# Two transformer layers with a mixture of experts: the order of all engines' instructions from another model of time

## The chip, the cores and the metric

The kernel runs on one core of a Trainium2 chip, in fp32. A core has five engines, each of which takes its own queue of instructions in order: TensorE (PE, with a separate queue for weight loads, PEld), VectorE (DVE), ScalarE (ACT), GpSimd (POOL) and SyncE (SP), which here issues most of the DMAs. The metric is device time in microseconds for one execution; a profile of one execution stands beside it.

## What is computed

The input is x of 4 batches x 512 tokens x 256. The two layers have this form (function bodies cut to what matters):

```python
# layer 0
xn = layernorm(x)
q, k, v = xn @ Wq.T + bq, xn @ Wk.T + bk, xn @ Wv.T + bv
context = (elu(q) + 1) * cumsum((elu(k) + 1) * v, axis=1) * SCALE
n0 = rms(xn) * norm_w
logits = n0 @ Wc.T / clip(temperature, 0.1)             # 512 genes
top_vals, top_idx = top_k(logits, 32)
expressed = sum(softmax(top_vals) * genes[top_idx])
x = x + context @ Wo.T + bo + tanh(expressed @ Wd.T) * n0 * (expressed @ Wu.T) * scale
# layer 1
xn = layernorm(x)
q, k, v = split(rms(xn) @ w_qkv.T)
w = exp(rms(k))
y = sigmoid(rms(q)) * (cumsum(w * v) / (cumsum(w) + 1e-6))
u, g = split(y @ w_swiglu.T)
x = x + xn + (u * silu(g)) @ w_out.T                    # hidden width 1024
scores = softmax(xn @ gate_w.T)                          # 16 experts, 2 are chosen
x = x + sum over the 2 experts of scores * swiglu(xn @ w_gate_up[e]) @ w_down[e]
      + swiglu(xn @ shared_gate_up) @ shared_down
```

All cumulative sums run along the 512 tokens of a batch.

## The kernel before

The 2048 tokens are 16 tiles of 128. The whole kernel is one function, `tile_two_layers`. It is made of generators, each of which writes a part of the program between two `yield`s:

- `layer0(b, i0, nt)`: layer 0 for nt tiles of batch b. Statistics and normalised rows (L201 to L214), their transposes on PE (`turn`, L221), logits of the genes (L289), four rounds of MAX8 and MATCH_REPLACE over 512 logits a tile on DVE for the 32 largest (L301, L302), the attention's products (`project`, L244), its elu and its cumulative sum (L257 to L280), the gene products (`express`, L316 to L334) and the output product with the residual add (L339, L342).
- `mix(b, i0, nt)`: the attention of layer 1 up to y, called yT (products L384, cumulative sums L421, yT L432), and the scores and the two chosen experts of each token (L435 to L456).
- `dense(busy)`: what depends on no routing: 8 halves of a batch (256 tokens), each of 11 chunks of hidden columns: three of the shared expert (from xn1T) and eight of the attention's swiglu (from yT). A chunk has four products into `gu` (L576), ACT and DVE or POOL work into `hid` (L580 to L587), and two products into `acc` (L596), issued two chunks behind. After the 11th, `acc` is added to x, which is kept on chip as `xs` (L607).
- `route()`: numbers of the rows in which each token's two copies stand, sorted by expert (products L486 and L487, then DVE). `scatter()`: 32 indirect DMAs from GpSimd that put the normalised rows into `xrows` in DRAM (L544). `load_experts()`: the experts' weights, into `wex`.
- `experts()`: 24 pairs of row tiles (47 tiles), each with its expert's number in a register: rows fetched (L711), transposed (L703), up products `pu` (L740), silu and product into `hb` (L748, L749), transposed again, down products `py` (L761), copied and written to `yrows` in DRAM (L770, L772).
- The tail: 32 indirect DMAs from GpSimd gather the rows of `yrows` into `ys` (L806), DVE adds them to `xs` with their weights (L817), and SP writes the output (L821, L826).

The order in the program comes from `together`, which takes steps from several generators in proportion to their lengths:

```python
    together(a(0, 0, 2))                                  # a is layer0, m is mix, d(n) is n steps of dense
    together(m(0, 0, 2), a(0, 2, 2))
    together(m(0, 2, 2), a(1, 0, 4), d(NC))               # NC = 11
    together(m(1, 0, 4), a(2, 0, 4), d(NC))
    together(m(2, 0, 4), a(3, 0, 4), d(NC))
    together(m(3, 0, 4), d(NC), (load_experts(), 17))
    together((route(), 8), d(5))
    together((scatter(), 33), d(14))
    run_all(islice(dd, 2 * NC - 19))                      # three more
    together((experts(), NP2 + 2))
    for step, _ in enumerate(dd):                         # the last 22 chunks, with gathers and adds between
```

So the program's text holds 66 of the 88 chunks ahead of the experts and 22 behind them, beside the gathers. The scatters, the expert weight loads and the gathers are `paced`: each depends on the `acc` product last written in the program, so that transfers are spread over the dense parts.

This text is not yet the order in which the engines run. The framework, Tile, collects the instructions with their dependencies (on data, and on the buffers of pools: three for `gu`, one for `acc`, four PSUM banks `pm` for the two layers, two for `pu`, one each for `pt` and `py`). At the end of a block a list scheduler goes through a model of time: when an engine is free, it gets, of the instructions whose inputs are ready in that model, the one that stands first in the program. The order found so is written into the engines' queues, with semaphores for the dependencies. On the chip the queues run in order: an instruction that waits holds up those behind it. In the kernel before, the model is the framework's default one, which the kernel doesn't choose.

Of the kernel before, what the change touches and what calls it, by code (L numbers as in the profile page):

```python
# [53 lines left out]
def tile_two_layers(  # L54
# [21 lines left out]
    out: bass.AP,  # L76
):
    nc = tc.nc
    V, S, G, T = nc.vector, nc.scalar, nc.gpsimd, nc.tensor

    const = ctx.enter_context(tc.tile_pool(name="const", bufs=1))
# [794 lines left out]
```

## Time and profile before

| | us |
|---|---|
| median of 3 runs | 591.41 (590.49 to 591.55) |
| the profiled execution's own time | 591.42 |
| its span, first to last instruction | 589.7 |
| PE busy by dense gu products (L576), from yT and from xn1T | 127.5 and 47.3 |
| PE busy by acc products (L596) | 67.4 |
| PE busy by pu (L740) and py (L761) of the experts | 63.8 and 44.5 |
| DVE busy by MAX8 (L301), 48 of its 64 | 32.9 |
| POOL busy by 32 scatters (L544) and 32 gathers (L806) | 31.0 and 30.7 |
| mean granted clock of PE | 0.975 of full |

How to read it: busy times of matmuls are sums of pipelined records, whose ends are modelled; they tell shares rather than limits. A group of instructions names the line of the kernel, the engine, the operation, what is written and what is read. "idle before" with a releaser says what ended the wait ahead of an instruction. An engine's idle time matters only where the chain of work that ends last runs through it. On that chain, followed back from the last instruction, PE has 61% of the span, DVE 21%, ACT 6% and POOL 4%.

### The profile page before, as it was taken

The page shows a single profiled execution, that of the slowest core. Times are in us where ns is not written, and L with a number is a line of the kernel's source. Part 1 is how long each engine was busy: PE and PEld are TensorE (multiplying, and loading weights), DVE is VectorE, ACT ScalarE, POOL GpSimd, SP SyncE. Part 2 cuts the span into 40 slices and gives each one's busy share as a digit, 9 for nine tenths or more (in the row PEclk, how much of TensorE's full clock was granted, in tenths as well). Part 3 has the DMA queues.
Part 4 walks back from the last instruction along what each step waited for, and adds up shares of the span by engine and source line. Part 5 has one row for each costly group of instructions (what it writes and reads, how often), then busy time and mean ns, then how long its engine had stood idle before and what let it go on. Part 6 is the DMA issues. An engine that isn't in the chain of part 4 may idle for free.

```text
span 589.7 us, 7350 instructions
## 1 busy us (share of the span) xinstructions
PE 539.4 (91%) x2384; PEld 393.0 (67%) x2384; DVE 373.1 (63%) x992; ACT 232.6 (39%) x528; POOL 173.9 (29%) x214
## 2 busy tenths in 40 slices
PE   3557989989999999999999999969999999999987
PEld 1334656558565685656877778857777777788876
DVE  3979999997896797967943785322222222235563
ACT  1453746653555625556265311103333333321111
POOL 1234232353221432224440326661000000006651
PEclk9788999999999999999999999989999999999999
DMA  4993000000000000000075602224233333114441
GB/s 159 375 377 140 1 1 1 2 0 1 1 1 0 1 1 1 1 1 1 1 236 170 182 2 80 91 86 136 90 108 107 108 108 98 55 63 125 126 133 46
DMA packets 38453, 47.39 MB, mean 80 GB/s; under 512 B 4016, under 2 KB 34960, under 8 KB 38160
## 3 DMA queue, kind: packets, MB, share of 16 engines
q1 hardware_dynamic: 35344, 38.53, 20.0%
q0 software_dynamic: 3072, 8.39, 4.6%
q8 instruction: 20, 0.33, 0.2%
q14 instruction: 17, 0.14, 0.1%
HBM read 28.30 MB, written 18.61 MB: 80 GB/s over the span
## 4 chain that ended last, share of the span: by engine, by line
PE 61%; DVE 21%; ACT 6%; POOL 4%; issue 3%; DMA 2%; SPq 0%; another core or an unknown queue 0%; POOLq 0%; ACTq 0%; DVEq 0%
PE gu L576 16%; PE pu L740 9%; PE acc L596 9%; PE py L761 7%; PE pm L384 5%; DVE rep L302 4%; DVE top L301 4%; PE pt L703 3%; POOL xrows L544 3%; PE pm L244 3%; PE pm L289 2%; PE pm L221 2%; PE pm L339 2%; DVE sums L430 2%; DVE sums L421 1%
## 5 line engine op out<-in xcount | busy, mean ns | idle before, releaser
L576 PE MATMUL gu<-yT,wugt 128*128 128x256 f32 x512 | 127.5, 385 | 0.0
L576 PEld LDWEIGHTS gu<-yT,wugt 128*128 128x128 f32 x512 | 96.0, 192 | 19.5 <-issue 7.2
L580 ACT ACTIVATE th<-gu 128x256 f32<-128x256 f32 (+1 forms) x88 | 33.0, 382 | 133.4 <-PE gu L576 85.9
L806 POOL DMA_INDIRECT ys<-yrows,slot x32 | 30.7, 961 | 145.4 <-PE gu L576 130.1
L596 PE MATMUL acc<-wot,hid 128*128 128x256 f32 x256 | 67.4, 386 | 5.9 <-DVE hid L584 5.5
L582 DVE SCALAR_TENSOR_TENSOR th<-th,gu 128x256 f32<-128x256 f32 (+1 forms) x88 | 36.1, 412 | 55.0 <-ACT th L580 46.3
L740 PE MATMUL pu<-wex,xgT 128*128 x188 | 63.8, 461 | 0.8 <-DMA xg<-xrows 0.8
L587 POOL TENSOR_TENSOR hid<-hid,th 128x256 f32<-128x256 f32 (+1 forms) x44 | 34.3, 782 | 101.1 <-ACT hid L586 97.8
L596 PEld LDWEIGHTS acc<-wot,hid 128*128 128x128 f32 x256 | 48.4, 192 | 15.5 <-DVE hid L584 5.9
L244 PE MATMUL pm<-xnT,wqkv 128*128 128x512 f32 (+1 forms) x120 | 46.7, 529 | 4.1 <-ACT lg L293 1.8
L576 PE MATMUL gu<-xn1T,sgu 128*128 128x256 f32 (+1 forms) x192 | 47.3, 382 | 1.4 <-ACT hid L586 1.3
L749 DVE TENSOR_TENSOR hb<-pu,hb 128x176 f32<-128x176 f32 x47 | 16.1, 342 | 51.0 <-ACT hb L748 51.0
L384 PE MATMUL pm<-w,xn1T 128*128 128x512 f32 (+1 forms) x128 | 45.7, 501 | 0.0
L761 PE MATMUL py<-wex,hgT 128*128 x188 | 44.5, 379 | 0.0
L761 PEld LDWEIGHTS py<-wex,hgT 128*128 128x128 f32 x188 | 35.6, 190 | 8.6 <-issue 0.2
L576 PEld LDWEIGHTS gu<-xn1T,sgu 128*128 128x128 f32 (+1 forms) x192 | 33.8, 181 | 9.5 <-ACT hid L586 2.6
L740 PEld LDWEIGHTS pu<-wex,xgT 128*128 128x128 f32 x188 | 32.0, 190 | 11.0 <-ACT xgT L717 1.0
L384 PEld LDWEIGHTS pm<-w,xn1T 128*128 128x128 f32 x128 | 24.6, 193 | 21.4 <-issue 17.9
L244 PEld LDWEIGHTS pm<-xnT,wqkv 128*128 128x128 f32 x120 | 23.8, 202 | 22.0 <-issue 13.2
L753 DVE COPY hgT<-pt 128x512 f32<-128x512 f32 (+1 forms) x24 | 16.3, 681 | 34.2 <-PE pt L703 34.2
L544 POOL DMA_INDIRECT xrows<-xn,slot x32 | 31.0, 969 | 23.8 <-DVE cpair L538 9.9
L301 DVE MAX8 top<-rep 128x8 f32<-128x512 f32 x48 | 32.9, 686 | 0.4
(162 smaller groups left out, 881.5 us busy)
## 6 DMA issues: line engine op xcount, KB each, us to landing
xrows<-zero SPq DMA_DIRECT2D x1, 6016.0 KB, 22.6
xg<-xrows SPq DMA_DIRECT2D x23, 256.0 KB, 2.7
yrows<-yg SPq DMA_DIRECT2D x23, 256.0 KB, 2.1
wex<-in_w_gate_up_dram SPq DMA_DIRECT2D x8, 704.0 KB, 4.8
xs<-in_x_dram SPq DMA_DIRECT2D x4, 512.0 KB, 7.7
wugt<-in_wug_dram SPq DMA_DIRECT2D x1, 2048.0 KB, 12.3
wex<-in_w_down_dram SPq DMA_DIRECT2D x4, 512.0 KB
out_dram<-xs SPq DMA_DIRECT2D x7, 256.0 KB, 2.7
```

Source lines behind the costliest of these rows:

```text
L244: T.matmul(pm, wqkv[:, h, c * P : (c + 1) * P], xnT[:, h, 0:W], start=(h == 0), stop=(h == NH - 1),)
L301: V.max(tp[:, 8 * r : 8 * r + 8], src)
L384: T.matmul(o[:, 0:n], xnT[:, h, i * P : (i + 1) * P], w1[:, h, at : at + n], start=(h == 0), stop=(h == NH - 1),)
L544: sc = G.indirect_dma_start(out=xrows, out_offset=bass.IndirectOffsetOnAxis(ap=slot[:, k, i : i + 1], axis=0), in_=xn1[:, i // NT, i % NT] ...
L576: T.matmul(gu[0:m, k], w[:, h, at : at + m], ins[which][:, h], start=(h == 0), stop=(h == NH - 1))
L580: S.activation(th[0:m], gu[0:m, 0], AF.Tanh, scale=0.5)
L582: V.scalar_tensor_tensor(th[0:m], th[0:m], 1.0, gu[0:m, 0], ALU.add, ALU.mult)
L587: G.tensor_tensor(hid[0:m], hid[0:m], th[0:m], ALU.mult)
L596: mm = T.matmul(acc[:, t], hid[0:m, t * P : (t + 1) * P], dw[0:m, dc], start=(n == 0 and t == 0), stop=(n == NC - 1), skip_group_check=True,)
L740: T.matmul(pg[:, 0 : 2 * NI], xT[:, i, h], wex[:, bass.ds(at[i] + h * 2 * NI, 2 * NI)], start=(h == 0), stop=(h == NH - 1),)
L761: mm = T.matmul(py[:, i * D : (i + 1) * D], hT[:, i, h], wex[:, bass.ds(at[i] + EW - (2 - h) * D, D)], start=(h == 0), stop=(h == 1),)
L806: G.indirect_dma_start(out=ys[:, asked], out_offset=None, in_=yrows, in_offset=bass.IndirectOffsetOnAxis(ap=slot[:, k, n : n + 1], axis=0) ...
```

## The change

One call is added at the start of `tile_two_layers`:

```diff
@@ -76,6 +76,8 @@
     out: bass.AP,
 ):
     nc = tc.nc
+
+    ctx.enter_context(tc.block(schedule_with_timeline_sim=True))
     V, S, G, T = nc.vector, nc.scalar, nc.gpsimd, nc.tensor
```

It puts the whole function into a block whose instructions are scheduled with the framework's finer model, a simulation of the time line, in place of the default one. The rule (of what is ready, the earliest in the program) stays, and so do the instructions, their operands, the pools and the dependencies. What differs is when the model holds an engine to be free and an input to be ready, and with that which instruction it picks: chunks of `dense` stand last in each stage's text but need no routing, so they are what fills an engine that has nothing earlier ready. The result is another order in each engine's queue. Line numbers of the changed kernel are higher by two.

## The prediction

> **What bounds the kernel now.** I read the page's first part, then busy time by stage, then the timeline around the last expert pair and at the end, and last the orders of the two programs.
>
> ```profile
> span 589.7 us, 7350 instructions
> PE 539.4 (91%) x2384; PEld 393.0 (67%) x2384; DVE 373.1 (63%) x992; ACT 232.6 (39%) x528; POOL 173.9 (29%) x214
> ```
>
> TensorE (PE) is idle for 50.3 us of 589.7. The stages say where (columns: stretch, its length, busy time and count of PE, PEld, DVE, ACT, POOL, granted clock, DMA share, GB/s):
>
> ```profile
> 0.00:86.00 86.00, 56.89 (x217) 34.73 (x218) 72.23 (x237) 38.30 (x84) 23.95 (x41) 0.88 0.51 180
> 86.00:145.00 59.00, 57.07 (x252) 37.84 (x251) 56.11 (x153) 31.87 (x70) 24.25 (x31) 1.00 0.00 1
> 145.00:219.00 74.00, 71.99 (x316) 48.45 (x314) 62.03 (x152) 39.03 (x89) 23.37 (x29) 1.00 0.00 1
> 219.00:299.00 80.00, 77.47 (x339) 52.23 (x338) 67.63 (x174) 43.33 (x94) 26.03 (x28) 1.00 0.05 14
> 299.00:345.00 46.00, 43.74 (x190) 32.03 (x189) 23.83 (x61) 20.57 (x55) 13.25 (x20) 1.00 0.55 166
> 345.00:406.00 61.00, 55.47 (x244) 47.17 (x243) 25.44 (x67) 7.34 (x20) 32.26 (x35) 0.94 0.23 80
> 406.00:526.00 120.00, 119.04 (x572) 90.92 (x571) 33.02 (x73) 43.79 (x96) 0.00 (x0) 1.00 0.31 97
> 526.00:590.00 64.00, 57.69 (x266) 49.65 (x265) 32.84 (x79) 8.34 (x23) 30.75 (x32) 0.98 0.35 101
> ```
>
> The start loses 29 us of PE; after it PE is 97% busy with VectorE (DVE) close behind (84 to 95%) up to 299 us. Then come the last mix, route and scatter (345 to 406), the experts, and a tail of 64 us in which PE still works 57.7. That work hides the gathers of the expert rows, which begin only after the last expert row is written (columns: start, us, engine, line):
>
> ```profile
> 525.65 0.37 ACT L770 COPY yg<-py 128x256 f32<-128x256 f32 x1 [1.36 <-PE py L761]
> ...
> 529.31 0.98 POOL L806 DMA_INDIRECT ys<-yrows,slot  x1 [128.23 <-PE gu L576]
> ...
> 548.48 0.94 POOL L806 DMA_INDIRECT ys<-yrows,slot  x1 [0.30 <-issue]
> 549.73 0.94 POOL L806 DMA_INDIRECT ys<-yrows,slot  x1 [0.30 <-issue]
> ...
> 576.28 0.95 POOL L806 DMA_INDIRECT ys<-yrows,slot  x1 [0.40 <-PE acc L596]
> ...
> 579.54 0.48 DVE L817 SCALAR_TENSOR_TENSOR xs<-ys,cpair,xs 128x256 f32<-128x256 f32 x1 [0.93 <-DMA ys<-yrows,slot]
> ...
> 585.54 0.69 DVE L607 TENSOR_TENSOR xs<-acc,xs 128x512 f32<-128x512 f32 x1 [1.29 <-PE acc L596]
> ```
>
> To see: 3.9 us from the last down product (its matmul ends near 525.4) to the first gather; 1.25 us from gather to gather when nothing holds them; 3.3 us from the last gather to its add; 3.5 us from the end of the last residual add (586.2) to the end. The gathers alone take 31 x 1.25 = 38.8 us, which today lie beside dense matmuls.
>
> **What the Trainium skill says.** "DMA: Bandwidth & Descriptors", section "SWDGE vs HWDGE vs iDMA": for a DMA issued from GpSimd, software on that engine computes the descriptors. The trace agrees: POOL is held 0.95 us a gather. "TensorE: Matmul & The Clock Gate", section "Part 1: The HAM clock gate": after an idle window of about 3.4 us matmuls run at half clock until some 3.4 us of work have passed. The trace agrees: four acc records that elsewhere span 1.03 us took 2.07 after an idle of 5.46.
>
> ```profile
> 394.83 2.07 PE L596 MATMUL acc<-wot,hid 128*128 128x256 f32 x4 [5.46 <-DVE hid L584]
> ```
>
> **The change, part by part.** Every instruction is kept but for six more activation-table loads (1.28 us each, on an engine that is 39% busy: nothing taken; 7.7 us if all stood on the path). SP's queue keeps its order but for the expert weight loads among themselves (8.4 MB that have over 60 us to land), POOL's that of scatters and gathers. What moves is the dense layer. A chunk is four gu and two acc products: eight gu records in 1.73 us and four acc records in 0.865, so 2.595 us of PE; there are 88. Each matmul at its back-to-back spacing in this trace (0.865 us for 512 columns, 0.595 for 352, 0.46 for 272, 0.4325 for 256, 0.11 for a 128-wide transpose) gives 517.5 us of work in either kernel. "Lag" is the time at a landmark less the work issued before it. Before: first logits of batch 1 done, 85.9 - 46 = 40; last turn of batch 2's rows, 144.7 - 100.9 = 44; of batch 3's, 219.0 - 172.2 = 47; last mix, 298.9 - 247.8 = 51; route products, 344.6 - 289.0 = 56; first expert product, 407.4 - 342.4 = 65; last matmul, 585.5 - 517.5 = 68. Then 4.2 us to 589.7.
>
> Chunks issued before these landmarks, old and new order: batch 2, 11.3 and 14.5; batch 3, 22.3 and 25.5; last mix, 35.0 and 50.8; route, 45.3 and 63.5; first expert product, 65.3 and 84.7. The old order keeps nearly two halves (57 us) for behind the experts. The new one puts its last three chunks between the first expert pairs and nothing behind the last down product: PE has 18 chunks, 47 us, more to do before route, and none in the tail.
>
> Tail: 3.9 + 38.8 + 3.3 + 0.5 (add) + 0.7 (last residual add, now behind the gathered adds) + 3.5 = 50.7 us with PE empty. The adds, 0.48 us, fit between gathers; the dense products that pace the gathers are long done. Bounds: 41 if the 0.30 gaps vanished, 54 if landings slow.
>
> Start, to 86 us: DVE sets it. Two tiles' top-32 are interleaved, and statistics and normalising of other batches stand ahead of batch 0's mix; they filled waits behind it before. Three chunks run in PE's gaps. I take the lag as it was, 40, bounds 34 to 44.
>
> Batch 1: five chunks stand ahead of the first tile's transposes and five more ahead of the third tile's logits. Work up to these is 84.6 us, 38.6 after the landmark at 46; at 1.02 (PE's busy 206 us against 202 of work from 86 to 299) that is 86 + 39 = 125, where DVE got them at 104.7. DVE then has rows of 38.7 us by mean duration; over the kernel those rows sum to 429 against 373 busy, 0.87, so 33.7 us, against 25 us of PE almost without chunks (the second half's yT is not made). End at 126 + 33.7 = 159.7 with 109.0 done: lag 51 for 44.
> Batch 2, the same: 39 x 1.02 = 40 to the logits, 1 to DVE, then 44.4 x 0.87 = 38.6 of DVE against 32 of PE: 239 with 179.8 done, lag 59 for 47.
> Batch 3: 25 chunks are free and the order takes them, so PE is full for 82.6 x 1.02 = 84 us up to the turns of q and k (323); then 18 us of DVE to the last out product and 8 to the normalised rows, with 23 us of PE inside: 349.5, 288.9 done, lag 61.
> Last mix: 47.3 of PE against 30 of DVE, plus 4 of stalls as before: route products at 401, lag 65.
> Route and scatter: 11.0 us to the first scatter, 31 x 1.27 = 39.3, 4.6 to land, 3.3 for xg: 58, beside 56 of PE work; before it took 61 with 5 of held scatters. First expert product 459.
> Experts: the same products at 4.97 us a pair; both pu tiles now stand together with one more turn ahead of the hidden turn, which covers ACT and DVE better, so no gain and no loss. 125 of work in 127: last matmul 586.
> Sum: 586 + 50.7 = 636.7 of span. The profiled run was 591.42 with a span of 589.70, 1.7 around it, and the median of the runs 591.41; so 638 us, 7.9% more.
>
> **Rivals.** (A) The front loses nothing: the order keeps DVE and PE so well fed that lag at the last matmul is 51. For it: the chunks in the start's gaps; against: no chunks in the second half of two stages. 517.5 + 51 + 50.7 + 1.7 = 621. (B) The stages alternate worse: waits of over 3.4 us behind a tile's top-32 bring the half clock at 2.5 us each (the eight gu and four acc records after 394.83 lost that), some six times: 653. (C) The other side, faster: the new order drains the start. Place: PE before 86 us; price: a us of span per us of lag; it decides below a lag of 21.5 at the last matmul (517.5 + 21.5 + 50.7 = 589.7), and 17 would give 587. For it: 29 us of idle PE there; against: PE's first matmul comes at 9.6 us, DVE is full from 45 us on, and its work there is no less. (D) Gathers begin before all of yrows is written and the tail shrinks to some 20 us: 607. Against: the first gather in the new POOL queue still waits for every hardware DMA queue. That nothing changes is excluded by the two orders.
>
> **Numbers.** Forecast 0.62 (own range 629 to 647), A 0.17, B 0.15, C 0.02, D 0.04. Range 618 to 655: it leaves out C, D and ends of the others. A measurement here tells 0.2%, 1.2 us, from no change: faster 0.02, same 0.01, slower 0.97.
>
> **What would show it.** Right: the last py near 586, then 32 gathers 1.25 us apart and PE empty for 48 us or more; PE's share near 85%; route products near 401; batches 1 and 2 each ending in a stretch in which PE is 80 to 90% busy. Wrong: dense products behind the last py or a gather before it (D), route products before 385 (A), a granted clock well under 0.95 between 86 and 350 us (B).

## The result, and the profile after

The changed kernel takes 689.09 us (685.58 to 692.75, four runs), the kernel before 591.34 (590.49 to 591.55) beside it: a ratio of 1.166, interval 1.160 to 1.172. The profiled execution is the slowest of the four, 692.75, with a span of 691.0. The forecast was 638 with a range up to 655: slower as forecast, but by 98 us and not by 47. The four runs of the changed kernel spread over 7.2 us, and most versions below ran once, so smaller differences between those are not read.

The first lines of the page, after:

```profile
span 691.0 us, 7313 instructions
PE 555.4 (80%) x2384; PEld 407.6 (59%) x2384; DVE 373.3 (54%) x992; ACT 242.1 (35%) x534; POOL 169.1 (24%) x214
PEclk9678999995999988999999999995799999999555
```

PE has the same 2384 matmuls. It is idle for 135.6 us where it was idle for 50.3, and busy for 16 us more, as part of its work now runs at a lower clock (0.898 in the mean, 0.975 before). (The 67.4 us that the table of before gives for the acc products are those of the attention's chunks alone; all of L596 took 92.6.) The third line shows where: near the start, at the ends of batches 1 and 2 (of the slices of 17 us each, the tenth, and the fifteenth with the sixteenth), at 466 to 500 us, and in the last three slices.

Busy time by stretch, after, with the columns of the prediction:

```profile
0.00:86.00 86.00, 48.94 (x168) 30.45 (x169) 58.84 (x210) 42.23 (x81) 20.89 (x37) 0.82 0.52 180
135.00:160.00 25.00, 20.37 (x76) 10.73 (x74) 19.41 (x60) 14.45 (x31) 7.74 (x12) 0.89 0.00 0
160.00:190.00 30.00, 25.82 (x93) 16.98 (x94) 18.67 (x49) 9.37 (x19) 7.60 (x9) 0.75 0.00 1
245.00:275.00 30.00, 23.66 (x104) 18.34 (x105) 23.37 (x41) 11.77 (x26) 11.35 (x14) 0.83 0.00 1
440.00:460.00 20.00, 20.00 (x95) 17.37 (x93) 7.32 (x21) 1.99 (x6) 14.85 (x16) 1.00 0.27 93
460.00:480.00 20.00, 6.34 (x14) 3.77 (x12) 0.85 (x2) 0.38 (x1) 15.15 (x16) 0.63 0.30 105
```

Three things to see. The first 86 us have 49 fewer matmuls and 27 fewer DVE instructions than before. The ends of batches 1 and 2 run at a clock of 0.75 and 0.83, with DVE below 80%. And at 460 us, in the middle of the scatters, TensorE goes from full to a third, from one 20 us stretch to the next, while GpSimd (POOL) issues 16 scatters in both.

The tail, from the timeline of after, is the one that was forecast:

```profile
638.72 1.10 PE L763 MATMUL py<-wex,hgT 128*128 x4 [0.61 <-DVE hgT L755]
...
644.36 0.98 POOL L808 DMA_INDIRECT ys<-yrows,slot  x1 [163.38 <-DMA yrows<-yg]
...
683.28 0.95 POOL L808 DMA_INDIRECT ys<-yrows,slot  x1 [0.30 <-issue]
...
686.88 0.69 DVE L609 TENSOR_TENSOR xs<-acc,xs 128x512 f32<-128x512 f32 x1
```

The last down product ends at 639.8, 32 gathers follow, and the last residual add stands behind them: 51.2 us with PE empty, where the sum gave 50.7.

Measured as the prediction did, by lag (time less the PE work issued), the two kernels compare so. "Forecast" is the prediction's own chain.

| landmark | before | forecast | after | error that this step added |
|---|---|---|---|---|
| first logits of batch 1 | 40 | 40 | 52.6 | 12.6 |
| end of batch 1 | 44 | 51 | 70.6 | 7.0 |
| end of batch 2 | 47 | 59 | 86.3 | 7.7 |
| rows of the last mix | 51 | 61 | 89.0 | 0.7 |
| route products | 56 | 65 | 93.4 | 0.4 |
| first expert product | 65 | 66.3 | 120.0 | 25.3 |
| last matmul | 68 | 68.5 | 122.3 | 0.1 |
| end of span (behind the last matmul) | 4.2 | 50.7 | 51.2 | 0.5 |

The last column sums to 54.3 us, which is the measured span less the forecast's 636.7. So four steps carry the error: the start, batch 1, batch 2, and route with scatter.

### The profile page after: what moved, and what is told of

The parts are those of the page before. It is cut to its first block, busy times and chain, and to the rows that moved or that the text cites. A ratio compares the mean times of both kernels' runs of the same rounds, so it can differ in the third digit from the quotient of the medians.

```text
span 691.0 us, 7313 instructions
## 1 busy us (share of the span) xinstructions
PE 555.4 (80%) x2384; PEld 407.6 (59%) x2384; DVE 373.3 (54%) x992; ACT 242.1 (35%) x534; POOL 169.1 (24%) x214
## 4 chain that ended last, share of the span: by engine, by line
PE 63%; DVE 13%; ACT 7%; another core or an unknown queue 4%; POOL 4%; DMA 4%; issue 3%; SPq 1%; POOLq 0%; DVEq 0%; ACTq 0%
PE gu L578 19%; PE acc L598 9%; PE pu L742 8%; PE py L763 6%; PE pm L386 5%; POOL ys L808 4%; PE pm L246 4%; PE pm L291 4%; PE pt L705 3%; DMA wot<-in_wout_dram 2%; PE pm L326 2%; DVE sums L432 2%; DVE sums L423 2%; DVE rep L304 1%
## 5 line engine op out<-in xcount | busy, mean ns | idle before, releaser
L578 PE MATMUL gu<-yT,wugt 128*128 128x256 f32 x512 | 130.1, 396 | 9.8 <-DVE yT L434 6.0
L578 PEld LDWEIGHTS gu<-yT,wugt 128*128 128x128 f32 x512 | 100.9, 199 | 29.2 <-DVE yT L434 8.2
L589 POOL TENSOR_TENSOR hid<-hid,th 128x256 f32<-128x256 f32 (+1 forms) x44 | 32.4, 740 | 126.0 <-ACT hid L588 126.0
L742 PE MATMUL pu<-wex,xgT 128*128 x188 | 59.9, 459 | 0.0
L246 PE MATMUL pm<-xnT,wqkv 128*128 128x512 f32 (+1 forms) x120 | 48.3, 541 | 1.0 <-DVE sums L423 1.0
L386 PE MATMUL pm<-w,xn1T 128*128 128x272 f32 (+1 forms) x128 | 44.8, 493 | 0.7 <-ACT xn1T L374 0.7
L742 PEld LDWEIGHTS pu<-wex,xgT 128*128 128x128 f32 x188 | 33.8, 190 | 14.4
L578 PEld LDWEIGHTS gu<-xn1T,sgu 128*128 128x128 f32 (+1 forms) x192 | 35.7, 187 | 6.8 <-issue 0.2
L763 PEld LDWEIGHTS py<-wex,hgT 128*128 128x128 f32 x188 | 33.8, 190 | 5.5 <-ACT hb L750 1.1
L291 PE MATMUL pm<-wct,xnT 128*128 128x512 f32 x64 | 34.4, 671 | 0.5 <-ACT xnT L239 0.5
```

Of the source, the lines that this page charges most:

```text
L246: T.matmul(pm, wqkv[:, h, c * P : (c + 1) * P], xnT[:, h, 0:W], start=(h == 0), stop=(h == NH - 1),)
L291: T.matmul(pl, xnT[:, h, i * P : (i + 1) * P], wct[:, h], start=(h == 0), stop=(h == NH - 1))
L386: T.matmul(o[:, 0:n], xnT[:, h, i * P : (i + 1) * P], w1[:, h, at : at + n], start=(h == 0), stop=(h == NH - 1),)
L578: T.matmul(gu[0:m, k], w[:, h, at : at + m], ins[which][:, h], start=(h == 0), stop=(h == NH - 1))
L589: G.tensor_tensor(hid[0:m], hid[0:m], th[0:m], ALU.mult)
L742: T.matmul(pg[:, 0 : 2 * NI], xT[:, i, h], wex[:, bass.ds(at[i] + h * 2 * NI, 2 * NI)], start=(h == 0), stop=(h == NH - 1),)
```

## The experiments

All times are to be held against 591.1 to 591.8 us of the kernel before on the same chips.

**The tail alone.** The default order, but the last 22 chunks issued ahead of the experts:

```diff
+    left = len(list(dd))
     together((experts(), NP2 + 2))
...
-    for step, _ in enumerate(dd):
+    for step in range(left):
```

> The kernel before, default order, with the last 22 chunks written ahead of the experts and nothing but gathers and adds behind them. Theory (the tail is worth what its dense work hid): 57 us of PE work leave a tail of 64 us, which becomes 51 with PE empty, and are paid ahead of the experts, 44 to 47 us more: 636. Rival (PE had room ahead of the experts, so the chunks are taken in at a part of their price): below 615.

Measured: 633.47, so 42 us for the empty tail. The prediction's price for it, 50.7 less the 4.2 that stood behind the last matmul before, 46.5, holds within 5 us in another order too.

**Is the hole at 460 us chance?** The changed kernel once more, unedited:

> The changed kernel once more, unaltered. In its first trace PE lost 27 us between the route products (430 us) and the first expert product (513 us), with ScalarE waiting 13 and 16 us for nothing that the trace names while GpSimd issued the scatters. Theory A (scatters delay the signals between the engines, a matter of chance): the total within 1% of 689, the stalls again inside the stretch of the scatters and nowhere else, but at other instructions or of another length. Theory B (the order itself, a chunk's down product too close behind its up product): the same stalls at the same instructions, within 1 us.

Measured: 691.5. ACT's timeline of this run around the scatters:

```profile
468.71 0.38 ACT L582 ACTIVATE th<-gu 128x256 f32<-128x256 f32 x1 [12.95 <-remote]
485.57 0.94 ACT L582 ACTIVATE th<-gu 128x256 f32<-128x256 f32 x3 [16.48 <-remote]
```

In the first execution (timeline of after):

```profile
458.49 1.89 PE L578 MATMUL gu<-yT,wugt 128*128 128x256 f32 x8
459.78 0.96 POOL L546 DMA_INDIRECT xrows<-xn,slot  x1 [0.30 <-issue]
468.85 0.38 ACT L582 ACTIVATE th<-gu 128x256 f32<-128x256 f32 x1 [12.95 <-remote]
469.72 0.42 DVE L586 TENSOR_TENSOR hid<-gu,th 128x256 f32<-128x256 f32 x1
470.20 2.08 PE L598 MATMUL acc<-wot,hid 128*128 128x256 f32 x4 [9.83 <-issue]
475.13 0.59 PE L578 MATMUL gu<-yT,wugt 128*128 128x256 f32 x1 [0.72 <-issue]
479.33 0.58 PE L578 MATMUL gu<-yT,wugt 128*128 128x256 f32 x1 [2.22 <-issue]
480.02 0.96 POOL L546 DMA_INDIRECT xrows<-xn,slot  x1 [0.30 <-issue]
485.71 0.94 ACT L582 ACTIVATE th<-gu 128x256 f32<-128x256 f32 x3 [16.48 <-remote]
```

The waits 12.95 and 16.48 repeat to the digit: no chance. Every `gu` product ahead of ACT's `th` at 468.85 had ended by 460.4; ACT waits 8 us more, for a releaser that the trace can't name ("remote"), and the `th` of the product of 458.49 comes only with the three from 485.71 on. PE's 9.8 us follow from this: the profile says "issue", but the acc product at 470.20 starts 0.06 us after the `hid` made from that `th` (469.72 and 0.42). What PE loses of its own is later: single matmuls of 0.6 us stand apart, with idle times of 0.7 to 2.2 us between them. POOL alone goes on: its 32 scatters keep 1.27 us from start to start. A wait for instructions to be loaded it was not: the DMA queues of kind "instruction" moved nothing from 446 to 498 us, and both engines stopped and went on within that time.

**The scatters as the cause.** The changed kernel without the 32 scatters:

```diff
-    together((scatter(), 33), d(14))
+    run_all(islice(dd, 14))
```

> The changed kernel with its 32 scatters left out, so that the experts read rows of zeros, with the same instructions otherwise. Theory A (the scatters delay the signals of PE and ScalarE): the loss of 27 us between route and experts goes, 662 to 666 us. Theory B (the loss is in the order of up and down products there): the two engines still stall, 685 or more.

Measured: 659.54. The hole is gone; lag stays at 88.1 from 420 us on, where the changed kernel's goes from 93.4 to 120.0. Of the 32 us of lag between them, 5 lie ahead of the route (the order changed there a little too), and 27 go with the scatters.

**Does it follow a fixed instruction, or the number of scatters?** 24 tiny copies on ACT at the start, which move every later instruction of ACT in its queue:

```diff
+    spare = const.tile([P, 1], F32, name="spare")
+    [S.copy(spare, ones[:, 0:1]) for _ in range(24)]
     load_x(0)
```

> The changed kernel with 24 copies of one column ahead of everything on ScalarE, in its wait for the input; the order is otherwise the same. Theory I (the stalls beside the scatters hang on how many instructions ScalarE's queue has run): they move or go, and the time changes by over 5 us. Theory S (they hang on the scatters, begun 16 and 27 of them in): the same two stalls of 13 and 16 us, 688 to 694 us.

Measured: 692.0. Neither theory as it was written: ACT's long waits have other lengths (17.85 and 10.91 us), the holes begin after the 16th and 18th scatter and the rest lies at the end of the row, but the lag that the row adds is again 26.6 us. Where the hole opens depends on details; what the row costs didn't.

**Breaking the row.** Four POOL additions (3.16 us) after the 8th, 16th and 24th scatter, and the next scatter behind them:

```diff
+                if i % 8 == 7 and (k, i) != (1, NTT - 1):
+                    for _ in range(4):
+                        op = G.tensor_tensor(rest, ones[:, 0:HB], ones[:, HB:L], ALU.add)
+                        tc.keep_in_program_order(op)
+                    held.append(op.ins.name)
...
```

> The changed kernel with four additions on GpSimd (some 3 us) behind the 8th, 16th and 24th scatter, the other engines' instructions as before. Theory P (scatters in a row without a pause hold up the signals of PE and ScalarE, and a pause lets them through, as where the kernel before makes a scatter wait for PE): PE's loss between the route products and the first expert product falls from 27 us to under 10, 664 to 676 us in all. Theory S (they hold them up from about the 16th on whatever is between): a loss of 27 or more, 688 to 700 us.

Measured: 670.73, 18 us under the changed kernel's median although POOL has more to do. POOL's timeline shows a pause, the windows what became of the hole:

```profile
462.10 0.96 POOL L549 DMA_INDIRECT xrows<-xn,slot  x1 [0.30 <-issue]
463.08 3.16 POOL L567 TENSOR_TENSOR rest<-ones 128x256 f32<-128x256 f32 x4
466.39 0.98 POOL L549 DMA_INDIRECT xrows<-xn,slot  x1 [0.15 <-issue]
```
```profile
460.00:480.00 20.00, 20.00 (x95) 17.37 (x94) 7.36 (x17) 2.74 (x8) 16.44 (x20) 1.00 0.22 76
```

PE is full in the 20 us in which it had 6.3. What is left, lag from 92.9 to 99.9, is mostly a wait of 4.6 us for the expert rows, as the scatters now end later. So a row of scatters without a pause is what holds ACT and PE up; a pause after every eighth nearly cures it. By what means the row does it no run shows.

A pause also lowers the rate of the scatters: 32 took 48.6 us here and 39.4 in the changed kernel. The traces part the two. In each run with all chunks the 88 `th` follow the 88 `gu` products in order, and outside the row of scatters a `th` most often starts 0.04 to 0.1 us behind its product. The latest one beside the scatters, by the longest row (scatters less than 1.5 us from start to start):

| run | longest row | all 32 took, us | latest `th` behind its product, us |
|---|---|---|---|
| without scatters, at their place | 0 | | 0.04 |
| with pauses | 8 | 48.6 | 1.2 |
| `front_fine` (below) | 12 | 43.7 | 6.4 |
| before | 14 | 43.9 | 9.3 |
| `back_fine` (below) | 18 | 44.8 | 12.4 |
| after | 32 | 39.4 | 27.9 |

At nearly the same rate, 43.7 to 44.8 us, the delay doubles from a row of 12 to one of 18: the length of the row counts. The other runs fit: a row of 11 gives 4.9, rows of 12 give 6.1 and 6.4, of 14 8.5 and 9.3, of 32 27.9 to 28.5.

The kernel before has the beginning of the same hole (timeline of before):

```profile
373.56 0.96 POOL L544 DMA_INDIRECT xrows<-xn,slot  x1 [2.23 <-PE gu L576]
...
393.48 0.94 ACT L580 ACTIVATE th<-gu 128x256 f32<-128x256 f32 x3 [9.53 <-remote]
393.78 0.96 POOL L544 DMA_INDIRECT xrows<-xn,slot  x1 [2.79 <-remote]
```

There the pacing waits still broke the row: a scatter waited 2.2 us for PE at 373.56, after the 12th. PE's hole came 13 scatters later, with 5.5 us of idle time, and the row was parted again: the 27th scatter waited 2.8 us. It is the idle of 5.46 that the prediction shows, and which its step on route called "held scatters". Would a pause help the kernel before as well? One, after the 24th:

> The kernel before, default order, with one pause on GpSimd (four additions, some 3 us) behind the 24th of the 32 scatters, just ahead of the place where PE lost 5.5 us and then ran at half clock. Theory P (a row of scatters without a pause holds up the signals): that idle goes, PE loses under 2 us in the stretch of the scatters, and the total is 583 to 588. Rival (GpSimd's row is the later chain there, so that the pause only moves the fetch of the experts' rows): 590 to 595.

Measured: 593.92 (592.48 to 595.42), ratio 1.0041 with an interval of 1.0029 to 1.0053: the rival was right. PE's waits at this place:

```profile
PE pt L718 <- DMA xg<-xrows: 3.4, 1, 3.4
PE acc L611 <- DVE hid L599: 2.6, 1, 2.6
```

Its idle time falls from 5.5 to 2.6 us and a wait of 3.4 for the first expert rows takes its place: in the kernel before, POOL's row is itself the later chain, so slowing it gains nothing.

**Which half of the kernel pays?** The finer model only up to the end of batch 3's stage (a block closed by `front.close()` after `first.close()`), and, the other way round, only behind it:

> The finer model for the block from the start through the stage of batch 3, the default model for the rest. Theory (what the front's order costs stays to the end, as every later part is full of PE work or bound by its own chain): the changed kernel's lag at 280 us is 86 and that of the kernel before 50, so 36 us more, 625 to 629, with lag about 86 at the end of the front. Rival (the four to five chunks drawn forward there are given back later): 600 to 615.

> The default model through the stage of batch 3, the finer one for last mix, route, scatter, experts and tail. Theory (its two prices are the uncovered tail, 42 us by the run with the last chunks written ahead, and some 20 us of stall beside the scatters): 648 to 656. Rival (the stall belongs to the place that the scatters have in the changed kernel): 630 to 640.

Measured: 640.02 and 640.27. In the first, lag is 82 at 300 us, much as in the changed kernel (86); the 33 chunks of that block are used up by then, PE has nothing to fill with until 360 us (lag 98), and the total lands 11 us above the expected range. In the second, lag at the route products is 55 (56 before), a hole of 10 us opens after 15 scatters, and the tail is 51 us. These are two losses of 49 us each. That they sum to the 98 of the whole is luck in part: by the table of lags, the changed kernel loses 38 us up to the rows of the last mix (89.0 for 51) and the rest behind, and some 16 of the 49 in the first run come from its own lack of chunks up to 360 us.

The same with the block from batch 1's stage on:

> The default model through the end of batch 0's first half, the finer one from the stage of batch 1 on. Theory (the start costs the changed kernel 12 us, most of it ScalarE's 7.9 us on the DMA of the weights that it halves): 675 to 681. Rival (batch 1 waits for another thing and takes the gain back): 686 to 692.

Measured: 688.41. The start is repaired (lag 40.0 at 80 us), yet lag at 200 us is 65.6 against 70.6, and the total lies within the runs of the changed kernel. Of the 12.6 us that the table books on the start, 5 are left at 200 us; the rest is lost there in either case.

**Do the chunks drawn forward cost the front, or fill it?** The first product of each chunk keeps its place in the program:

```diff
-                    T.matmul(
+                    mm = T.matmul(
...
+                    if k == 0 and h == 0:
+                        tc.keep_in_program_order(mm)
```

> The changed kernel with each of the 88 chunks held behind the product that stands before it in the program. Theory (what the finer model's order costs is almost all in the chunks that it draws forward; beside that it costs 12 us in the start, where ScalarE halves the output weights too early and waits 7.9 us for their DMA): 600 to 606, with the lag of PE at 100 us at 53 as in the changed kernel and then parallel to the kernel before. Rival (the order of VectorE, ScalarE and the mixes costs of its own in every stage): over 615.

Measured: 645.67; the rival was right. Lag at the route products rises from 93 to 111, and PE waits 21.5 us for POOL's `hid`; what is won comes from the tail, where 22 chunks lie beside the gathers again, and from a hole of only 4.6 us. So holding the chunks back doesn't free the front: without them to fill in, PE is short of work there. Pinning only those behind the first 44:

> The changed kernel with the chunks from the stage of route on (the last 44) held behind the product that stands before them in the program, so that 22 stay behind the experts and 22 beside route and scatter. Theory (the uncovered tail and the stall go, the front's loss of 36 us stays and grows by some 12, as fewer chunks are left for the last mix): 624 to 638. Rival (the last mix loses what the tail gains): 655 or more.

Measured: 655.54, as the rival had it. The 44 free chunks are used up by 360 us and lag rises from 80 at 340 us to 119 at 420: the scheduler spends what it may spend as early as it can. With the default order up to batch 3's stage and the same pin (an `and g >= 44` in the condition above) behind it:

> The default model through the stage of batch 3 and the finer one behind it, with the last 44 chunks held behind the product that stands before them in the program, so that 22 stay beside route and scatter and 22 behind the experts. Theory (in the second half the uncovered tail and the stall are all that the finer order costs): within 1% of the kernel before, 586 to 597 us. Rival (the last mix or the experts lose besides, as the last mix did where the finer front stood ahead of it): 605 to 625.

Measured: 599.48 (596.82 to 601.67), ratio 1.0126, interval 1.0076 to 1.0176, just above the expected range. Keeping 22 chunks for the tail and others beside the scatters, where the longest row is now 12, gives back 41 of the 49 us that the finer model cost behind batch 3; 8 remain unexplained.

**Is it the order of mix and layer 0 itself?** No chunks in the stages of batches 1 and 2 (22 of them left out), once with each model:

```diff
-        for half in range(2 * B):
+        for half in range(2, 2 * B):
...
-    together(m(0, 2, 2), a(1, 0, 4), d(NC))
-    together(m(1, 0, 4), a(2, 0, 4), d(NC))
+    together(m(0, 2, 2), a(1, 0, 4))
+    together(m(1, 0, 4), a(2, 0, 4))
```

> The finer model, with the dense work of batch 0 (22 chunks, which stood in the stages of batches 1 and 2) left out, so that batch 0 has no dense part in its output. Measured is the stretch from a batch's first logits to its last out product, 80 us for batch 1 and 75 for batch 2 in the changed kernel, 60 and 67 in the one before. Theory Q (the chunks in the queues ahead of the top-32 hold up VectorE): 55 to 60 us in both batches, as in the default order without these chunks. Theory O (the finer model's order of mix and layer 0 is slower of itself): 8 us or more above the default order without these chunks.

> The kernel before with the same 22 chunks left out. The stretches from first logits to last out product, with VectorE alone to bound them: 52 to 58 us in both batches (theories Q and O alike); it is the measure for the run with the finer model.

Measured: 654.64 and 573.15. From the first logits of batch 1 to its last out product, finer first:

```profile
93.00:158.00 65.00, 41.98 (x142) 21.41 (x143) 50.26 (x135) 26.45 (x53) 14.82 (x20) 0.82 0.00 1
```
```profile
85.00:139.00 54.00, 40.73 (x144) 20.99 (x145) 49.20 (x134) 26.54 (x52) 14.38 (x19) 0.91 0.00 1
```

All five engines have the same work to within 1.3 us and need 65 us for it instead of 54; in batch 2 it is 65 instead of 57. With the chunks, batch 1's stretch is 80 us after and 60 before: so 11 of those 20 us come with the order of mix and layer 0 alone, and 9 only with the chunks in it. In batch 2 it is 75 after and 67 before, 8 in all, the same as without chunks.

A suspect was the alternation of two tiles' top-32 on DVE, which both lengthens the wait for a tile's result and splits it. Every tile's second round behind the end of the tile before it:

```diff
+                if r == 1 and ends:
+                    tc.add_manual_dep(mx8.ins, ends[-1],
+                        mybir.DependencyInfo(mybir.DependencyClass.NoSync, mybir.DependencyReason.DATA),
+                        reason="one tile's top-32 after the other's")
...
```

> As the run with the finer model and without the 22 chunks of batch 0 (whose dense part is missing in the output), with the second and later rounds of a tile's top-32 held behind the end of the tile before. Theory T (the alternation of two tiles' rounds on VectorE delays the first tile's result and all that follows): the stretch from a batch's first logits to its last out product falls from 65 to 58 us or less in batches 1 and 2. Rival (the rest of VectorE's order, which is late for the third and fourth tile, counts): 62 to 66.

> The changed kernel with a tile's top-32 held behind the end of the tile before in the same way, nothing left out. Theory T: three to four batches at 7 to 10 us each, 655 to 668. Rival (only the first tile's result moves, by 3 to 4 us, and other waits take its place): 680 to 692.

Measured: 655.46 without the 22 chunks (stretches of 64 and 66 us) and 685.89 with all of them, 3 us under the changed kernel's median and within its runs. The alternation isn't it. Which part of the order costs the 11 and 8 us stays open.

No version beat the kernel before.

## Why the prediction was right and wrong

**Right: the direction and the tail.** The two orders told that no chunk is left behind the last down product, and the sum from the spacing of gathers gave 50.7 us where 51.2 came. That step is some 42 us of the loss by itself (the run with the tail emptied in the default order). Experts ran in the 127 us forecast, the last mix and batch 3 within 1 us of the forecast.

**Wrong, and the largest term: "Route and scatter: 11.0 us to the first scatter, 31 x 1.27 = 39.3, 4.6 to land, 3.3 for xg: 58, beside 56 of PE work".** It took 83.1. (In the kernel before it took 62.8, from 344.6 to 407.4, and not the 61 that the step gives, the length of its window.) The scatters did go 1.27 us apart, and the 56 of PE work were there; that they lie beside each other was assumed, and the row of scatters stops ACT and PE. The clue stood in the profile of before: a `th` held for 9.53 us with its product done, and PE idle for 5.46 us behind it. The prediction took it for "held scatters", that is, POOL waiting on PE and not PE on POOL's row. In the new order the pacing waits, which had parted the row, are met long before, as the chunks are drawn forward, and lag grows by 26.6 us from the route to the first expert product where it grew by 9.

**Wrong: "I take the lag as it was, 40, bounds 34 to 44".** It was 52.6. The step looked at DVE alone. The new queue of ACT has the halving of the output weights ahead of batch 0's first gene copy (ACT in the timeline of after, then of before):

```profile
29.64 2.19 ACT L642 ACTIVATE wot<-wot 128x512 f32<-128x512 f32 x4 [7.90 <-DMA wot<-in_wout_dram]
32.56 0.56 ACT L320 COPY wT<-pm 128x512 f32<-128x512 f32 x1
```
```profile
25.14 0.59 ACT L318 COPY wT<-pm 128x512 f32<-128x512 f32 x1 [4.17 <-PE pm L316]
...
34.00 0.63 ACT L640 ACTIVATE wot<-wot 128x512 f32<-128x512 f32 x1
```

ACT waits 7.9 us for a weight that nothing needs yet, and the copy comes 7.4 us later. The order shows this without a run; it was not read off ACT's queue. The six more table loads, which the prediction priced at nothing on the mean load of ACT, count here too: up to 62 us there are nine where there were four, and the chain that ended last runs through six up to 106 us, 1.28 us each, where that of before has one up to 86. Two of those on the chain:

```profile
45.55 1.28 ACT L209 ACT_TABLE_LOAD   x1
47.06 1.28 ACT L328 ACT_TABLE_LOAD   x1
```

No run takes the loads away by themselves. The block that begins after the start gives these microseconds back, but most are lost again by 200 us, so this term alone explains little of the total.

**Wrong: the 38.7 x 0.87 = 33.7 us of DVE rows for batch 1, and 44.4 x 0.87 = 38.6 for batch 2.** The steps' ends came 7.0 and 7.7 us later than these allow. The factor takes DVE as always supplied, as it nearly was before (84 to 95% busy); in the new order each engine waits for the others (DVE 62% busy from 160 to 190 us). PE's busy time rose by 16 us in all, and this is rival B's mechanism, at a clock of 0.75 to 0.89 at the stage ends, beside the forecast's and not in place of it. An estimate from the three windows shown (the clock's shortfall times PE's busy time: 2.2, 6.5 and 4.0 us) puts 12.7 us of it there. Whether it makes the 7.0 and 7.7 us isn't shown: without the chunks, the finer order took 11 us more for batch 1 with only 1.3 us more of PE busy time. According to the Trainium skill, "TensorE: Matmul & The Clock Gate", section "Part 1: The HAM clock gate", matmuls run at half clock after an idle window of about 3.4 us, and this trace agrees: the four acc records at 470.20, behind 9.8 us of idle time, took 2.08 us, twice the 1.03 of others.

The range ended at 655 because it held the rivals one at a time. Much of what rival B priced, a late start and the hole came together. The hole itself, 25 us, was in none of them.

## What to carry to other kernels

An order that uses filler as soon as it is ready leaves none for the stretches that only DMAs set: look first at what is left beside gathers and scatters, as the empty tail alone cost 42 us here. Then read, for each engine's new queue, what stands at the front waiting for a load (ACT's 7.9 us here), since that is to be had without a run. And count table loads where their engine is on the chain, not by its mean load. When a wait in a trace has its producers done and no releaser named, find out what runs steadily at that moment before moving work beside more of it.

## What the runs showed of the hardware

A row of GpSimd's indirect DMAs, each 0.96 us of POOL and 1.27 us apart, added some 27 us of lag on PE when 32 (of 128 rows each) stood in a row, three times the same in the changed kernel and its variant; none when the row was parted every 8 by 3.16 us of other POOL work, or left out. ACT's start behind a finished product of PE came up to 1.2 us late in rows of 8, 6.4 in rows of 12, 9.3 in one of 14, 12.4 in one of 18 and 27.9 in one of 32. PE's own holes began after 12 to 18 scatters in a row in these runs. (With the chunks pinned the hole came after the 26th scatter and had 4.6 us, but there a wait of POOL had parted the row after the 12th, so it was the 14th in its row.) What in the row holds the other engines isn't shown, nor whether the 32 gathers of the tail, which are as close, would do the same to a PE that has work: PE was empty beside them in the changed kernel, and in the kernel before no more than 7 stood in a row.
